# The first stage of a hybrid convolution, scan and spectral kernel: the order of a planner against an order written out in the program

## The chip, the cores and the metric

The kernel runs on one core of one Trainium2 chip. The metric is device time in microseconds of one launch, as the median of several runs. A core has five engines with instruction queues of their own: PE (TensorE; PEld are its weight loads), DVE (VectorE), ACT (ScalarE), POOL (GpSimd) and SP (SyncE), which here issues all the transfers. Each engine works through its queue in order; it waits for others through semaphores.

## The reference, cut to what matters

The layer computes, in float32, on 4 images of 128 channels and 64 x 64 pixels:

```python
# layer 0, on the group-normalized image (groups of 4 channels)
feat = gelu(dwconv2d(x, conv1_w, conv1_b))                  # 3x3, per channel
ca = sigmoid(relu(feat.mean((2, 3)) @ ca1_w.T) @ ca2_w.T)   # a gate for each channel
feat = gelu(dwconv2d(feat * ca[:, :, None, None], conv2_w, conv2_b))
scores = sigmoid(einsum('bchw,oc->bohw', feat, head_w)[:, 0] + head_b[0])
final_scores = 0.7 * scores + 0.3 * sigmoid(10 * var(x, axis=channels, ddof=1))
sm = final_scores.reshape(B, 16, 4, 16, 4).mean((2, 4))     # 256 patches of 4 x 4
idx = argsort(-sm)                                          # patches in order of their score
# tokens (x + pe), layer-normalized, taken in that order, then a scan over them,
# an output projection, and back into the image's order
# layer 1: a second scan over 512-wide chunks and a spectral convolution, with
# filters M_phi_plus[i], M_phi_minus[i], M_u[i] of four branches i
y_soft = softmax(log_weights + gumbel)                      # weighs the four branches
```

The change lies in the part up to the ordered tokens, and in a preparation for layer 1: the four branches' filter matrices are scaled by the branch weights and added up.

## The kernel before

The kernel is a chain of three stages, written with a tile framework that gives out buffers from pools and puts in the waits. `layer0_front` is the first stage, `layer0_scan` the second, `layer1` the third. In stages two and three the program switches the framework's planner off (`tc.manual_schedule()`), so that each engine's queue has the program's order. In `layer0_front` the planner is on: it chooses the order of every queue.

`layer0_front` loops over the 4 images (`for b in range(NB)`). For each image:

- SP loads the image, `xs` (128 x 4096). DVE takes its statistics (`bn_stats`, L126), PE averages them over groups of four channels (`gs`), POOL raises to the power -0.5 (`rs`, L142), and DVE writes the normalized image into the bordered tile `xg` (L144).
- ACT lays the pixels out by patches (`xp1`, L149). PE transposes them, four 128 x 128 blocks at a time (`tp`, L164). For each of these eight blocks of four, DVE adds the position code (`x1`, L166) and takes statistics of both (`stx`, `st1`, L168 and L169). 64 aggregates follow (L171, L172), a `pow` on POOL (`r1`, L176), the product `m1` on DVE (L180), and 32 scalings of `x1` on ACT (L183).
- A convolution (`conv`, L94 to L109) has eight pieces of 128 x 512. In each, PE does four of the nine taps as products with diagonal matrices into a PSUM tile (L104) and DVE the other five as a chain of accumulates (L106): the first one reads the PSUM tile and writes an SBUF tile `sum`, of which there are three; the other four read and write `sum`. ACT applies a Gelu to `sum`. The first convolution's pieces give `f1`, with channel sums (L193).
- A small chain makes the gate: `mean`, `hid`, `hs`, `cap`, `ca` (L198 to L207). The gate is multiplied into the second convolution's weights (`d2b`, `w2b`). The second convolution gives `f2` (L215).
- PE makes the scores by 32 products (`sc`, L225); ACT and DVE finish them (L230 to L237). DVE ranks the 256 patches by comparison (L243 to L259) and writes the permutation `perm`. PE transposes it for later (L263), gathers the tokens in order by 32 products with it (`ranked`, L274), ACT evacuates (`xn`, L277), SP stores `xnt`.

Tiles of one tag share buffers. In pool `xp` every tag has one buffer (`xp1` and `f2` share the tag `patches`). PSUM pool `pm` has four buffers of one bank each, for the pieces of convolution, the transposes and the gathers; `ps1` has two.

`spectral_weights` is a generator that `layer0_front` advances with `next(matrices, None)`, six times at the start of each image but the first. Each step makes the summed filter matrices of one of 16 filters: SP loads `raw`, ACT does four scalings (L677), POOL three adds, a sum and a difference (L679, L695, L696), SP stores two `pq`. Ahead of them it makes the branch weights and the matrices `mue` from `mu` in one piece. The planner decides where these instructions lie in the queues; in the profile all of them are beside image 0.

Of the kernel before, what the change touches and what calls it, by code (L numbers as in the profile page):

```python
# [15 lines left out]
NB = 4  # L16
L = 4096
# [6 lines left out]
def layer0_front(ctx: ExitStack, tc, ident, half, w, x, xnt, perm_t, pqd, mud):  # L24
# [3 lines left out]


    nc = tc.nc  # L30
    cp = ctx.enter_context(tc.tile_pool(name="a_c", bufs=1))
    xp = ctx.enter_context(tc.tile_pool(name="a_x", bufs=1))
    sm = ctx.enter_context(tc.tile_pool(name="a_sm", bufs=2))
    pm = ctx.enter_context(tc.tile_pool(name="a_pm", bufs=4, space=PSUM))
    ps1 = ctx.enter_context(tc.tile_pool(name="a_p1", bufs=2, space=PSUM))

    def load(name, shape, src):
# [77 lines left out]
    matrices = spectral_weights(  # L115
        ctx, tc, w["sigma"], w["M_u"], w["M_phi_plus"], w["M_phi_minus"], w["log_weights"], w["gumbel"], pqd, mud
    )
    for b in range(NB):

        xs = xp.tile([128, L], F32, tag="xs", name="xs")  # L120
        nc.sync.dma_start(xs, x[b])
        for _ in range(6 if b else 0):
            next(matrices, None)
        st = sm.tile([128, 8, 6], F32, tag="st", name="st")
        for q in range(8):
            nc.vector.bn_stats(st[:, q, :], xs[:, bass.ts(q, 512)])  # L126
        mv = sm.tile([128, 2], F32, tag="mv", name="mv")
        nc.vector.bn_aggr(mv, st)

        gm = sm.tile([128, 1], F32, tag="gm", name="gm")  # L130
        sq = sm.tile([128, 1], F32, tag="sq", name="sq")
# [8 lines left out]
        nc.vector.tensor_scalar(sq, gs, 1e-5, None, ALU.add)  # L140
        rs = sm.tile([128, 1], F32, tag="rs", name="rs")
        nc.gpsimd.tensor_tensor(rs, sq, half[:, 0:1], ALU.pow)  # L142
        xg, inside = bordered("xg")
        nc.vector.tensor_scalar(  # L144
            inside, xs.rearrange("c (y x) -> c y x", x=64), gm, rs, ALU.subtract, ALU.mult
        )
        xp1 = xp.tile([128, L], F32, tag="patches", name="xp1")
        for oy in range(4):
            nc.scalar.copy(  # L149
                by_patch(xp1, oy), inside[:, oy::4, :].rearrange("c py (px ox) -> c py px ox", ox=4)  # L150
            )


        x1 = xp.tile([128, 2, 16, 128], F32, tag="x1", name="x1")
        stx = sm.tile([128, 2, 16, 6], F32, tag="stx", name="stx")
        st1 = sm.tile([128, 2, 16, 6], F32, tag="st1", name="st1")
        mvx = sm.tile([128, 2, 16, 2], F32, tag="mvx", name="mvx")
# [2 lines left out]
        for h in range(2):  # L160
            for oy in range(4):
                tp = pm.tile([128, 4, 128], F32, tag="mm", name="tp")
                for ox in range(4):
                    nc.tensor.transpose(tp[:, ox, :], patches[:, h, 4 * oy + ox, :], ident)  # L164
                o4 = bass.ts(oy, 4)
                nc.vector.tensor_tensor(x1[:, h, o4, :], tp, pe[:, h, o4, :], ALU.add)  # L166
                for o in range(4):
                    nc.vector.bn_stats(stx[:, h, 4 * oy + o, :], tp[:, o, :])  # L168
                    nc.vector.bn_stats(st1[:, h, 4 * oy + o, :], x1[:, h, 4 * oy + o, :])  # L169
            for o in range(16):  # L170
                nc.vector.bn_aggr(mvx[:, h, o, :], stx[:, h, o, :])  # L171
                nc.vector.bn_aggr(mv1[:, h, o, :], st1[:, h, o, :])  # L172
# [5 lines left out]
        )  # L178
        m1 = sm.tile([128, 2, 16], F32, tag="m1", name="m1")
        nc.vector.scalar_tensor_tensor(m1, mv1[:, :, :, 0], -1.0, r1, ALU.mult, ALU.mult)  # L180
        for h in range(2):
            for o in range(16):
                nc.scalar.activation(  # L183
                    x1[:, h, o, :], x1[:, h, o, :], AF.Identity, bias=m1[:, h, o : o + 1],
                    scale=r1[:, h, o : o + 1],
                )


        f1, inside1 = bordered("f1")
# [1 line left out]
        for i in range(8):  # L191
            h, oy = divmod(i, 4)
            nc.scalar.activation(  # L193
                inside1[:, 32 * h + oy : 32 * h + oy + 29 : 4, :], conv(xg, d1, w1, h, oy), AF.Gelu, bias=b1,
                accum_out=sums[:, i : i + 1],
            )
        mean = sm.tile([128, 1], F32, tag="mean", name="mean")
        nc.vector.tensor_reduce(mean, sums, AX, ALU.add)  # L198
        nc.vector.tensor_scalar(mean, mean, 1.0 / L, None, ALU.mult)
# [5 lines left out]
        nc.tensor.matmul(cap, ca2, hs, start=True, stop=True)  # L205
        ca = sm.tile([128, 1], F32, tag="ca", name="ca")
        nc.scalar.activation(ca, cap, AF.Sigmoid)  # L207
        d2b = xp.tile([128, PT, 128], F32, tag="d2b", name="d2b")
        nc.vector.tensor_scalar(d2b, d2, ca, None, ALU.mult)
        w2b = sm.tile([128, 9], F32, tag="w2b", name="w2b")  # L210
        nc.vector.tensor_scalar(w2b, w2, ca, None, ALU.mult)
        f2 = xp.tile([128, L], F32, tag="patches", name="f2")
        for i in range(8):
            h, oy = divmod(i, 4)
            nc.scalar.activation(  # L215
                by_patch(f2, oy)[:, 8 * h : 8 * h + 8],
                conv(f1, d2b, w2b, h, oy).rearrange("c py (px ox) -> c py px ox", ox=4), AF.Gelu, bias=b2,
            )


        sc = ps1.tile([128, 2, 16], F32, tag="one", name="sc")
        fpatch = f2.rearrange("c (h p o) -> c h o p", h=2, o=16)
        for h in range(2):
            for o in range(16):
                nc.tensor.matmul(  # L225
                    sc[:, h, o : o + 1], fpatch[:, h, o, :], head,
                    start=True, stop=True,
                )
        s1 = sm.tile([128, 2, 16], F32, tag="s1", name="s1")
        nc.scalar.activation(s1, sc, AF.Sigmoid, bias=head_b)  # L230
        s2 = sm.tile([128, 2, 16], F32, tag="s2", name="s2")
# [3 lines left out]
        score = sm.tile([128, 2], F32, tag="score", name="score")  # L235
        nc.vector.tensor_reduce(score, s1, AX, ALU.add)
        nc.vector.tensor_scalar(score, score, 1.0 / 16, None, ALU.mult)  # L237


        row = ps1.tile([128, 2, 128], F32, tag="one", name="row")  # L240
        for h in range(2):
# [6 lines left out]
        for h in range(2):  # L248
            more = sm.tile([128, 1], F32, tag="more", name="more")
            same = sm.tile([128, 1], F32, tag="same", name="same")  # L250
            junk = sm.tile([128, 256], F32, tag="junk", name="junk")
            mine = score[:, h : h + 1]
            nc.vector.tensor_scalar(junk, scores, mine, None, ALU.is_gt, ALU.add, accum_out=more)
            junk = sm.tile([128, 256], F32, tag="junk", name="junk")
            nc.vector.scalar_tensor_tensor(
                junk, scores, mine, before[:, h, :], ALU.is_equal, ALU.mult, accum_out=same
            )
            nc.vector.tensor_tensor(more, more, same, ALU.add)
            nc.vector.tensor_scalar(perm[:, h, :], index, more, None, ALU.is_equal)  # L259
        for h in range(2):  # L260
            tp = ps1.tile([128, 2, 128], F32, tag="one", name="tp1")
            for k in range(2):
                nc.tensor.transpose(tp[:, k, :], perm[:, k, bass.ts(h, 128)], ident)  # L263
            nc.vector.tensor_copy(perm_t[:, b, h, :], tp.rearrange("p k j -> p (k j)"))


        xn = xp.tile([128, 3 + L], F32, tag="xn", name="xn")
        nc.vector.memset(xn[:, 0:3], 0.0)
        ranked = xn[:, 3:].rearrange("c (r o) -> c o r", o=16)
        for o in range(0, 16, 2):  # L270
            ps = pm.tile([128, 2, 256], F32, tag="mm", name="ranked")
            for i in range(2):
                for h in range(2):
                    nc.tensor.matmul(  # L274
                        ps[:, i, :], x1[:, h, o + i, :], perm[:, h, :], start=h == 0, stop=h == 1
                    )
            nc.scalar.activation(ranked[:, o : o + 2, :], ps, AF.Identity, bias=nb, scale=ng)  # L277
        nc.sync.dma_start(xnt[b], xn)


NS = 16
# [344 lines left out]
def spectral_weights(ctx, tc, sigma, m_u, m_plus, m_minus, log_w, gumbel, pqd, mud):  # L626
# [19 lines left out]
    nc.vector.tensor_scalar(lw, lw, top, None, ALU.subtract)  # L646
    soft = cp.tile([128, 4], F32, name="soft")
    tot = cp.tile([128, 1], F32, name="tot")
    nc.scalar.activation(soft, lw, AF.Exp, accum_out=tot)
    nc.vector.reciprocal(tot, tot)  # L650
    nc.vector.tensor_scalar(soft, soft, tot, None, ALU.mult)
# [22 lines left out]
    def branch_sums(dst, src, weight):  # L674

        for i in range(4):
            nc.scalar.activation(dst(3 - i), src(i), AF.Copy, scale=weight(i))  # L677
        for i in range(1, 4):
            nc.gpsimd.tensor_tensor(dst(3 - i), dst(3 - i), dst(4 - i), ALU.add)  # L679

    mu = mp.tile([128, 4, 3, 128], F32, name="mu", bufs=1)
    for i in range(4):
        nc.sync.dma_start(mu[:, i], m_u[i].rearrange("k d e -> d k e"))
    mue = mp.tile([128, 4, 3, 128], F32, name="mue", bufs=1)
    branch_sums(lambda r: mue[:, r], lambda i: mu[:, i], lambda i: wt[:, i : i + 1])
    nc.sync.dma_start(mud, mue)
    yield
    for k in range(NK):
        raw = mp.tile([128, 2, 4, 128], F32, tag="raw", name="raw")
        nc.sync.dma_start(raw[:, 0], m_plus[:, k].rearrange("i d e -> d i e"))  # L690
        nc.sync.dma_start(raw[:, 1], m_minus[:, k].rearrange("i d e -> d i e"))
        sums = mp.tile([128, 2, 4, 128], F32, tag="sums", name="sums")
        branch_sums(lambda r: sums[:, :, r], lambda i: raw[:, :, i], lambda i: both[:, i, k : k + 1])
        pq = mp.tile([128, 2, 4, 128], F32, tag="pq", name="pq")
        nc.gpsimd.tensor_tensor(pq[:, 0], sums[:, 0], sums[:, 1], ALU.add)  # L695
        nc.gpsimd.tensor_tensor(pq[:, 1], sums[:, 0], sums[:, 1], ALU.subtract)  # L696
        for side in range(2):
            nc.sync.dma_start(pqd[k, side], pq[:, side])
        yield
# [673 lines left out]
```

## Time and profile before

| what | us |
|---|---|
| median of 3 runs | 21742.6 |
| lowest and highest run | 21742.6, 21744.73 |
| the profiled execution | 21746.66 |
| its span | 21744.9 |
| first stage: from the start to the last evacuation of `xn` | 607.5 |
| from one `xg` to the next (27.1, 201.5, 337.5, 472.3) | 174.4, 136.0, 134.8 |
| DVE, POOL, PE, ACT busy over the whole span | 20628.6, 20221.1, 17469.3, 15865.3 |
| DVE, PE, ACT, POOL busy in the first 640 us | 409.3, 428.3, 213.8, 126.2 |

The profile is of one execution. A span is the time from its first to its last instruction. In a group of instructions the columns are line, engine, operation, tiles out and in, shapes and number, then busy time in us and the mean of one in ns, then the idle time ahead of them and what ended it. In a timeline a row is start and length in us; instructions of one engine can overlap by a fraction, so lengths from start to start are the better measure of a queue. The first stage is 2.8% of the span.

### The profile page before, as it was taken

To read this page: it belongs to the slowest core of one execution; us is meant where nothing else is said; L and a number is where in the kernel's file an instruction comes from. 1 tells how busy PE (TensorE), PEld (TensorE's weight loads), DVE (VectorE), ACT (ScalarE), POOL (GpSimd) and SP (SyncE) were. 2 spreads that over 40 slices of the span, in tenths; PEclk is the share of its full clock that TensorE was granted. 3 is DMA by queue.
4 is the path that set the end of the run, shared out by engine and by line. 5 is a ranking of instruction groups with operands and counts; after the bars stand their busy time and mean duration, and the time that the engine had idled before them with its cause. 6 is when DMAs were issued, how large, how long until landed. Compare 5 with 4: busy or idle time off the path is not lost.

```text
span 21744.9 us, 291339 instructions
## 1 busy us (share of the span) xinstructions
PE 17469.3 (80%) x98516; PEld 7646.0 (35%) x98516; DVE 20628.6 (95%) x11808; ACT 15865.3 (73%) x29216; POOL 20221.1 (93%) x5679
## 2 busy tenths in 40 slices
PE   6788854565858888877768888869498899999999
PEld 3344421222323333333323333324143344434344
DVE  6788889999999999999999999999999999999993
ACT  3677767777777777777777777777777777877773
POOL 2677789999999999999999999999999999999993
PEclk7999966776979999998879999979699999999999
DMA  1455544555757777766667777757476777777775
GB/s 68 112 139 141 140 149 151 173 178 163 217 171 219 219 222 220 218 205 196 201 189 218 222 218 220 222 183 231 154 235 216 226 235 235 234 232 231 232 227 150
DMA packets 2420940, 4245.65 MB, mean 195 GB/s; under 512 B 795208, under 2 KB 1255024, under 8 KB 2416368
## 3 DMA queue, kind: packets, MB, share of 16 engines
q1 hardware_dynamic: 2419440, 4227.01, 63.6%
q8 instruction: 776, 12.71, 0.2%
q14 instruction: 724, 5.93, 0.1%
HBM read 3605.76 MB, written 620.24 MB: 194 GB/s over the span
## 4 chain that ended last, share of the span: by engine, by line
DVE 51%; POOL 23%; PE 9%; ACT 8%; issue 6%; DMA 2%; SPq 0%; DVEq 0%; POOLq 0%; ACTq 0%
DVE s L1155 44%; POOL v L1143 22%; ACT da L1152 5%; PE conv L1103 4%; DVE states L513 3%; DVE p L517 1%; PE yp L1172 1%; ACT f L505 1%; PE fin L1047 1%; PE y L529 1%; DMA dlb<-delta 1%; PE mm L422 1%; DMA yd<-ye 1%; PE conv L104 0%; DVE sum L106 0%
## 5 line engine op out<-in xcount | busy, mean ns | idle before, releaser
L1143 POOL TENSOR_TENSOR v<-u,dlb 128x2044 f32<-128x2044 f32 x4096 | 18333.8, 4536 | 68.1 <-DMA dlb<-delta 64.9
L1155 DVE TENSOR_TENSOR_SCAN s<-da,v 128x1024 f32<-128x1024 f32 x8192 | 18130.6, 2272 | 192.7 <-ACT da L1152 91.1
L1152 ACT ACTIVATE da<-dlb,at 128x511 f32<-128x511 f32 x16384 | 11302.4, 690 | 2235.1 <-DVE s L1155 1774.2
L1103 PE MATMUL conv<-strip,tok 128*128 128x512 f32 (+3 forms) x20480 | 8609.0, 550 | 5.9 <-DMA strip<-in_phi 5.8
L1172 PE MATMUL yp<-s,c 128*32 128x256 f32 x65536 | 5030.9, 438 | 3065.5 <-DVE s L1155 1601.6
L1103 PEld LDWEIGHTS conv<-strip,tok 128*128 128x128 f32 x20480 | 3666.5, 191 | 4104.4 <-issue 3705.1
L1172 PEld LDWEIGHTS yp<-s,c 128*32 128x32 f32 x65536 | 1992.5, 121 | 6865.7 <-issue 1822.2
L1147 ACT COPY v<-vf 128x4 f32<-128x4 f32 x4096 | 812.7, 198 | 2234.0 <-DVE s L1155 2228.7
L491 POOL TENSOR_TENSOR v<-dx,bcb 128x1024 f32<-128x1024 f32 x512 | 1207.2, 2358 | 433.6 <-DVE states L513 427.3
L1047 PE MATMUL fin<-conved,pq 128*128 128x512 f32 (+1 forms) x3200 | 1411.8, 536 | 11.1 <-ACT sum L1068 4.1
L513 DVE TENSOR_TENSOR_SCAN states<-f,v 128x1024 f32<-128x1024 f32 x512 | 1175.9, 2297 | 176.1 <-ACT f L505 126.5
L505 ACT ACTIVATE f<-dt,an 128x255 f32<-128x255 f32 x2048 | 973.6, 476 | 420.0 <-DVE states L513 369.2
L1178 ACT COPY ye<-yp 128x512 f32<-128x512 f32 x2048 | 1185.0, 579 | 16.7 <-PE yp L1172 15.4
L529 PE MATMUL y<-p,ident 128*128 128x512 f32 x2048 | 1004.8, 619 | 152.3 <-DVE p L517 147.4
L1114 ACT COPY conved<-conv 128x512 f32<-128x512 f32 x1344 | 778.0, 579 | 327.7 <-PE conv L1103 326.4
L517 DVE TENSOR_TENSOR p<-states,bcb 128x1024 f32<-128x1024 f32 x512 | 627.0, 1225 | 38.2 <-PE y L535 0.4
L529 PEld LDWEIGHTS y<-p,ident 128*128 128x128 f32 x2048 | 368.3, 195 | 684.0 <-issue 356.3
L1047 PEld LDWEIGHTS fin<-conved,pq 128*128 128x128 f32 x3200 | 528.0, 193 | 221.3 <-issue 160.7
L422 PE MATMUL mm<-ow,yg 128*32 128x128 f32 x2048 | 280.5, 296 | 106.8 <-ACT om L426 105.3
L1063 DVE TENSOR_TENSOR xo<-xo,fin 128x512 f32<-128x512 f32 x32 | 21.3, 667 | 306.8 <-PE fin L1055 306.8
L422 PEld LDWEIGHTS mm<-ow,yg 128*32 128x32 f32 x2048 | 235.3, 138 | 212.5 <-ACT om L426 128.4
L356 PE MATMUL mm<-xin,taps 128*128 128x512 f32 x512 | 237.2, 606 | 28.3 <-DVE f L335 14.0
(242 smaller groups left out, 5932.4 us busy)
## 6 DMA issues: line engine op xcount, KB each, us to landing
dlb<-delta SPq DMA_DIRECT2D x4096, 512.0 KB, 4.1
strip<-in_phi SPq DMA_DIRECT2D x1536, 448.0 KB, 4.8
yd<-ye SPq DMA_DIRECT2D x2048, 256.0 KB, 4.1
bcb<-bcd SPq DMA_DIRECT2D x1024, 256.0 KB, 4.2
strip<-in_phi SPq DMA_DIRECT2D x1024, 256.0 KB, 4.4
pq<-pqd SPq DMA_DIRECT2D x1088, 64.0 KB, 3.8
yt<-yd SPq DMA_DIRECT2D x4096, 4.0 KB, 3.4
pq<-pqd SPq DMA_DIRECT2D x256, 128.0 KB, 4.0
```

Of the source, the lines that this page charges most:

```text
L491: nc.gpsimd.tensor_tensor(v, ready[n][2][:, :, bass.ts(i, SUB)].unsqueeze(1).broadcast_to((128, 2, 2, SUB)), bc[:, 0].unsqueeze(2).broadca ...
L505: nc.scalar.activation(factors[j % 2][:, a, k, 1:], ready[n][1][:, k, SUB * i + 1 : SUB * i + SUB], AF.Exp, scale=an[:, k, 2 * g + a : 2 * ...
L513: nc.vector.tensor_tensor_scan(states.rearrange(flat), factors[j % 2].rearrange(flat), v.rearrange(flat), 0.0, ALU.mult, ALU.add)
L517: nc.vector.tensor_tensor(p, states, bc[:, 1].unsqueeze(2).broadcast_to((128, 2, 2, SUB)), ALU.mult)
L529: nc.tensor.matmul(t.rearrange("p k t -> p (k t)"), ident, p[:, a].rearrange("p k t -> p (k t)"), start=g == 0 and a == 0, stop=False, ski ...
L1047: nc.tensor.matmul(fin[:, bass.ds(c0, w)], pq[:, n, :], u[:, bass.ds(c0, w)], start=begin and n == 0, stop=end and not partly, skip_group_ ...
L1103: nc.tensor.matmul(ps[:, skip:], tok[:, 1 - r if side else r, j, :], strip[:, bass.ds(c0 - lo, TS - skip)], start=src == sources[0] and j ...
L1143: nc.gpsimd.tensor_tensor(v[:, :, :, 1:], ready[0][:, :, 1:].unsqueeze(1).broadcast_to((128, VD, 2, TS - 1)), dl[:, :, 1:].unsqueeze(2).br ...
L1152: nc.scalar.activation(da[:, h, 1:], dl[:, d % VD, 1:], AF.Exp, scale=at[:, h, d : d + 1])
L1155: nc.vector.tensor_tensor_scan(s[:, d % GD].rearrange("p h t -> p (h t)"), da.rearrange("p h t -> p (h t)"), v[:, d % VD].rearrange("p h t ...
L1172: nc.tensor.matmul(yp[i // 2][bass.ts(q, 32), i % 2], c[:, h, t], s[:, :, h, t], start=h == 0, stop=h == 1)
L1178: nc.scalar.copy(ye, yp[j].rearrange("p i d t -> p i t d"))
```

## The change

The planner is switched off in `layer0_front`, and the order is written out. The loop's body becomes two generators: `tokens(b)`, from the load of `xs` to `m1`, and `ordered(b, ...)`, from the first convolution to the store. A small class advances them by pieces. Image 0's `tokens` runs whole; then for each image its `ordered` pieces alternate with the `tokens` pieces of the next image and with steps of `matrices`:

```python
    first = Pieces(tokens(0))
    first.go()
    for b in range(NB):
        rest = Pieces(ordered(b, *first.result))
        first = Pieces(tokens(b + 1)) if b + 1 < NB else Pieces(iter(()))
        first.go(1)                 # load of the next image
        for _ in range(4):
            rest.go(2)              # two pieces of the first convolution
            next(matrices, None)
        first.go(1)                 # statistics of the next image
        rest.go(2)                  # gate
        first.go(1)                 # its group sums and pow
        rest.go(4)                  # gate into the weights; three pieces of the second convolution
        first.go(1)                 # xg and the layout by patches
        next(matrices, None)
        rest.go(6)                  # five pieces, eight scores
        for n in (1, 1, 1, 1, 1, 1, 2, 2):
            first.go(1)             # four transposes with their statistics
            rest.go(n)              # scores, score arithmetic, ranking, permutation, gathers
        first.go()
        rest.go()
```

The order in which each engine gets its instructions follows from this. On DVE, behind the last accumulate of the second convolution, it is: four blocks of statistics, the score arithmetic, 32 aggregates and a block, the ranking, a block, the permutation's copies, a block, a block, 32 aggregates, `m1`. On ACT four of the 32 scalings of `x1` stand behind each Gelu of the first convolution, and four scalings of a filter behind every second one. On SP the load of the next image stands behind the store of the last one.

Buffers: `pm` has six instead of four. `xs` has 3 + 4096 columns and shares its buffer with `xn`; `xp1`, `f2` have their own; `x1` has two.

```diff
-    pm = ctx.enter_context(tc.tile_pool(name="a_pm", bufs=4, space=PSUM))
+    pm = ctx.enter_context(tc.tile_pool(name="a_pm", bufs=6, space=PSUM))
...
-        xs = xp.tile([128, L], F32, tag="xs", name="xs")
+        xs = xp.tile([128, 3 + L], F32, tag="xs", name="xs")[:, 0:L]
...
-        xp1 = xp.tile([128, L], F32, tag="patches", name="xp1")
+        xp1 = xp.tile([128, L], F32, tag="xp1", name="xp1")
...
-        x1 = xp.tile([128, 2, 16, 128], F32, tag="x1", name="x1")
+        x1 = xp.tile([128, 2, 16, 128], F32, tag="x1", name="x1", bufs=2)
...
-        for h in range(2):
-            for o in range(16):
-                nc.scalar.activation(
-                    x1[:, h, o, :], x1[:, h, o, :], AF.Identity, bias=m1[:, h, o : o + 1],
-                    scale=r1[:, h, o : o + 1],
-                )
+            for o in range(4 * i, 4 * i + 4):
+                h, o = divmod(o, 16)
+                nc.scalar.activation(
+                    x1[:, h, o, :], x1[:, h, o, :], AF.Identity, bias=m1[:, h, o : o + 1],
+                    scale=r1[:, h, o : o + 1],
+                )
+            yield
...
-        f2 = xp.tile([128, L], F32, tag="patches", name="f2")
+        f2 = xp.tile([128, L], F32, tag="f2", name="f2")
...
-        xn = xp.tile([128, 3 + L], F32, tag="xn", name="xn")
+        xn = xp.tile([128, 3 + L], F32, tag="xs", name="xn")
```

In `spectral_weights` a step is taken ahead of the softmax, the matrices `mue` are made in three slices through the buffers of the filters, and each filter's `raw` is loaded one filter ahead:

```diff
+    yield
     nc.scalar.activation(soft, lw, AF.Exp, accum_out=tot)
...
-    mu = mp.tile([128, 4, 3, 128], F32, name="mu", bufs=1)
-    for i in range(4):
-        nc.sync.dma_start(mu[:, i], m_u[i].rearrange("k d e -> d k e"))
-    mue = mp.tile([128, 4, 3, 128], F32, name="mue", bufs=1)
-    branch_sums(lambda r: mue[:, r], lambda i: mu[:, i], lambda i: wt[:, i : i + 1])
-    nc.sync.dma_start(mud, mue)
-    yield
-    for k in range(NK):
+    for k in range(3):
+        raw = mp.tile([128, 2, 4, 128], F32, tag="raw", name="mu")[:, 0]
+        nc.sync.dma_start(raw, m_u[:, k].rearrange("i d e -> d i e"))
+        sums = mp.tile([128, 2, 4, 128], F32, tag="sums", name="mue")[:, 0]
+        branch_sums(lambda r: sums[:, r], lambda i: raw[:, i], lambda i: wt[:, i : i + 1])
+        nc.sync.dma_start(mud[:, :, k], sums)
+
+    def fetch(k):
         raw = mp.tile([128, 2, 4, 128], F32, tag="raw", name="raw")
         nc.sync.dma_start(raw[:, 0], m_plus[:, k].rearrange("i d e -> d i e"))
         nc.sync.dma_start(raw[:, 1], m_minus[:, k].rearrange("i d e -> d i e"))
+        return raw
+
+    ahead = fetch(0)
+    yield
+    for k in range(NK):
+        raw, ahead = ahead, fetch(k + 1) if k + 1 < NK else None
```

## The prediction

> **What bounds the kernel now.** The change touches only the first stage: read instruction by instruction, the built kernels agree on every engine behind the last `xnt` store. So I cut out the chain of waits of the first 700 us. Start, length, what:
>
> ```profile
> 472.26 2.43 DVE xg L144
> 474.76 1.07 ACT xp L149
> 475.87 1.13 PE tp L164 x4
> 477.03 0.69 DVE x L166
> 499.58 5.41 POOL r L176
> 505.24 12.43 ACT x L183 x32
> ...
> 540.16 30.73 PE conv L104 x64
> 570.89 13.66 PE sc L225 x64
> 586.11 1.24 PE row L244 x4
> ...
> 591.95 14.29 PE ranked L274 x62
> 606.27 1.21 ACT xn L277
> ```
>
> This is image 3, and images 1 and 2 look the same: a serial run through normalize, transpose and statistics on DVE, a `pow` on POOL, two convolutions, scores, ranking, gathers. From one `xg` to the next are 136.0 and 134.8 us, and the last image takes 135.2. No engine is full in it. The first image is longer. The busy times of the two stretches (PE, PEld, DVE, ACT, POOL):
>
> ```profile
> 201.50:337.50 136.00, 105.43 (x304) 63.42 (x304) 92.47 (x268) 43.79 (x75) 6.00 (x2) 0.77 0.08 31
> 27.00:201.50 174.50, 105.56 (x304) 63.03 (x304) 126.64 (x287) 73.63 (x144) 102.72 (x86) 0.73 0.35 114
> ```
>
> POOL's 102.7 us there are the spectral weights, all 16 of them, which the scheduler puts beside image 0. What they do to DVE is in the groups of that stretch, then of image 2 (337.5 to 472.3), where POOL is idle:
>
> ```profile
> L106 DVE SCALAR_TENSOR_TENSOR sum<-f,w2b,sum 128x512 f32<-128x512 f32 x32 | 41.5, 1307 | 0.8
> L106 DVE SCALAR_TENSOR_TENSOR sum<-f,w2b,conv 128x512 f32<-128x512 f32 x8 | 5.9, 737 | 8.8 <-PE conv L104 5.8 <-ACT f L215 3.0
> ```
>
> ```profile
> L106 DVE SCALAR_TENSOR_TENSOR sum<-f,w2b,sum 128x512 f32<-128x512 f32 x32 | 23.6, 750 | 0.8
> ```
>
> The same accumulate is 1307 ns beside POOL and 750 without it; the form whose second operand is in PSUM stays at 737. Last, the timeline of DVE at the start of the second convolution of image 2:
>
> ```profile
> 411.04 0.75 DVE L106 SCALAR_TENSOR_TENSOR sum<-f,w2b,conv 128x512 f32<-128x512 f32 x1 [5.65 <-PE conv L104]
> 411.82 3.11 DVE L106 SCALAR_TENSOR_TENSOR sum<-f,w2b,sum 128x512 f32<-128x512 f32 x4
> 414.85 0.74 DVE L106 SCALAR_TENSOR_TENSOR sum<-f,w2b,conv 128x512 f32<-128x512 f32 x1
> ```
>
> A piece of convolution written in plain order costs DVE 3.81 us (411.04 to 414.85) and waits 5.65 us for PE's first piece. Where the scheduler interleaves two pieces, as in the first convolution, the same ten take 6.67 (384.96 to 391.63), 3.3 each.
>
> **What the Trainium skill says.** SBUF — State Buffer, section "Who interferes with whom": a DVE instruction with two SBUF inputs contends with a GpSimd instruction that reads SBUF, one with a single SBUF input does not. The trace agrees (1307 and 750 against 737). TensorE: Matmul & The Clock Gate, section "What's actually happening": an idle array restarts at half clock for some 3.4 us. The trace agrees in kind: the first piece of a convolution takes 5.65 us, the later ones about 3.7 (29.91 us for 8). Perfetto Trace Analysis, section "Optimization Strategy": regimes with different bottlenecks may gain from interleaving. That is what is done here; how far it pays is the question.
>
> **The change, part by part.** Durations are start to start from the timelines of the profiled execution (us).
>
> *Taken off the path.* Image b+1's normalize, transposes and statistics move under image b. Today the front costs from 472.26 to 505.2, 33.0, and is followed by the first convolution. Three fronts go (images 1 to 3); image 0's stays as it is, up to 60.6. Counted: 8 blocks of one add and eight statistics, 2.15 each; 2 times 32 aggregates, 2.13; `xg` 2.9 with its border; 4 ACT copies of 1; 5.45 `pow`.
>
> *What the tail becomes.* Take t = 0 at the last accumulate of the second convolution. Gelu to 0.85; PE has the first 16 scores behind it, does 8 scores (3.4), 4 transposes (0.7), 8 scores, and then the transposes for block 4, so DVE's blocks end at 2.15, 4.3, 7.35 and 11.5. Score arithmetic to 12.4, aggregates 14.5, block 5 to 16.65, diagonal and PE `row` to 18.3, ranking to 21.3. PE: permutation transposes and block 7's to 23.3, gathers and block 8's to 38.5 (62 gathers take 14.07 in image 2), the next convolution's first piece 42.2, DVE starts at 42.3. DVE's own blocks, the wait for `pow` (5.45, in front of `m1`) and the border end at 38.4: the stall is hidden behind the gathers. Today: 440.34 to 472.26 is 31.9, then the front of 33.0. So 64.9 become 42.3.
>
> *Given back.* (a) DVE's queue is now in plain order: 8 pieces of the first convolution at 3.81 are 30.5 (bunched today: 32.4 with 5.2 of next statistics in it). (b) Those statistics (5.2) stand behind it and the next image's group sums on PE and DVE inside the gate's chain: 9.3 from the last accumulate to PE's next start, against 3.1 today after the Gelu. (c) The second convolution has `xg` in its queue, which waits for POOL's `rs`, already there: 5.7 + 8 x 3.81 + 2.9 = 39.1, and 41.6 with a weight beside it (below); today 35.1. (d) The spectral weights are spread, five to an image. One keeps POOL for about 6.5 (3.43 + 1.6 + 1.6), in which DVE's piece of 3.81 becomes 6.4 (119.83 to 126.26), a loss of 2.6. Three fall into the first convolution (7.8), the fourth behind its last Gelu, into the gap, one into the second convolution (2.6). Their ACT part (4 x 0.4) and the 32 scalings of `x1` (12.4), now four behind each Gelu, fit: 3.2 a piece against DVE's 3.8. Nothing is behind them but ACT's own Gelus, and three `sum` tiles cover them.
>
> Period of images 1 and 2: 38.3 + 9.3 + 41.6 + 42.3 = 131.5, against 135.4: 4 gained each.
>
> *Image 0.* Its first convolution meets the weights' setup. DVE waits some 4 for ACT's softmax exponential behind the fourth Gelu, then 4 of small operations (to 84.5). The three slices of `mu` go one after another: SP is in order, and each load stands behind the previous slice's store, which waits for POOL. Per slice ACT 1.6, POOL 1.5, issue 0.5 to 1, landing 3.7: about 8. ACT reaches its fifth Gelu at 103 instead of 85; DVE, three pieces ahead, stalls from 96. With the two loads of weight 0 behind it, PE starts the second convolution at 117.7, today at 107.1. Then 41.6 + 42.3: DVE starts image 1's first convolution at 201.6, where today `xg` begins at 201.5 and that convolution's bulk at 234.3. 33 gained so far.
>
> *Image 3.* No front beside it: 38.3 + 4.5 + 36.2 (5.7 + 30.5) + 30.6 (scores 7, ranking 6, gathers 16, evacuation) = 109.6. Today from the same point (505.2) to 607.5 is 102.3: 7.3 lost, by plain order and contention.
>
> *SP's queue.* `xs` of image b+1 shares its buffer with `xn` of b-1, so its load waits for that store (8.0 in the chain), and the weights' loads queue behind it. It has the 38 of a first convolution; the loads are one weight ahead. I cost this at nothing; without that cover it would be the landing, 9.2. The layer-1 weight loads move ahead of the second `xs` and take the place of `mu`'s 0.8 MB: nothing. Table loads stay four an image. PSUM's six buffers instead of four only let PE run ahead.
>
> Sum: stage end 201.6 + 2 x 131.5 + 109.6 = 574.2, against 607.5: 33 less. The profiled execution is 21746.66 (span 21744.9), hence 21713; the median of the runs is 4.1 lower, so **21710**.
>
> The cost that the trace doesn't show is contention when weights trickle in. Lower bound 1 per weight (POOL waiting for ACT in between), upper 3.3 (piece at 6.4, and POOL itself at 8 when both fight): 13 weights, so -21 to +9 on the sum; I take 2.6 because it was measured with POOL full. The plain piece could be 3.56, as at 425 to 436, where only one operation is interleaved: up to 16 less over 64 pieces; slower than 3.81 has no reason with PE ahead, bar PE's clock (0.73 to 0.81 granted here). The `mu` chain: 8 either way.
>
> **The rivals.** *Better cover* (30 in 100). Contention 1.4 per weight and pieces at 3.6: 33 + 16 + 13 = 62 gained, 21681. For it: POOL shows idle gaps as soon as ACT feeds it singly. Against: the contended pieces of image 0 are steadily 5.8 to 6.4 long.
>
> *ACT starved by the weights* (8 in 100), the slower case. Each weight's four scalings stand between Gelus. In image 0 today ACT waits for loads:
>
> ```profile
> L677 ACT ACTIVATE sums<-raw,both 128x256 f32<-128x256 f32 x64 | 27.8, 496 | 50.4 <-DMA raw<-in_M_phi_minus 28.1 <-POOL pq L696 11.9 <-POOL pq L695 7.1
> ```
>
> A load is issued behind the store of two weights earlier: POOL 6.7, two stores 2, two loads 1, landing 3.7 and ACT 1.7 make 15 for two weights, and DVE's four pieces give 15 to 20. If the stores hold SP as the pairs at 135 and 161 did (7 to 9), each weight is late by 5 and a Gelu, then DVE, with it: 16 x 5 = 80 lost, 47 net, 21790. It decides from 4.8 per weight. Against: those long stores came when SP had four in a row waiting for POOL.
>
> *No change at all* (within the middle case): if the tail's interleaving costs PE or DVE some 8 more per image, 33 shrinks to nothing, 21743.
>
> **How the numbers follow.** Some 0.2% (43 us) is what a measurement of this kernel can tell from no change. My forecast (62 in 100) gains 10 to 43, within it; better cover gains 44 to 75; starved loses over 43. Hence 0.30 faster, 0.62 same, 0.08 slower; the range 21670 to 21750 leaves out the starved case and the ends of the others.
>
> **What would show it.** In the changed profile: `xg` of images 1 to 3 inside the second convolution; DVE `sum` starting about 201, 333 and 464; 42 between a second convolution's end and the next first; last `xn` near 574; accumulates near 1.3 us only beside POOL; ACT waiting for `mu` twice, 5 each. Wrong if ACT waits for `raw` at most weights, if the tail is over 48, or if spans behind the stage differ by over 10.

## The result and the profile after

| us | before | after |
|---|---|---|
| median, 18 runs each | 21745.47 | 21705.62 |
| lowest to highest | 21741.26 to 21753.52 | 21699.14 to 21713.26 |
| profiled execution (span) | 21746.66 (21744.9) | 21708.22 (21706.5) |
| last `xn` evacuated | 607.5 | 562.7 |
| span behind that point | 21137.4 | 21143.8 |

The ratio is 0.9982 (95% interval 0.9975 to 0.9988): 40 us or 0.18% less. Forecast were 21710 and a stage end of 574.2. The time is met within 5 us, but by misses that partly cancel: the stage gained 44.8 instead of 33, and the rest of the program shows 6 more in the profile, where nothing was forecast. The forecast also started from a median of 21742.6, of 3 runs, where 18 runs give 21745.47; as a gain, 33 was forecast and 40 came. That the time was met so closely is in part luck.

In the changed kernel `conv` accumulates at L107 (before L106), PE multiplies at L105, scores at L237, gathers at L289. The chain of waits of the first 700 us, cut down (start, length, what):

```profile
176.23 4.12 PE ranked L289 x16
180.79 10.36 PE ranked L289 x48
191.16 3.48 PE conv L105 x8
...
233.03 4.76 DVE st L127 x8
...
242.74 5.20 PE conv L105 x8
...
495.42 29.35 PE conv L105 x64
524.77 13.66 PE sc L237 x64
...
545.61 15.81 PE ranked L289 x64
561.45 1.21 ACT xn L292
```

Behind a gather comes the next image's convolution at once (191.16). Where `xg`, layout, transposes and `pow` stood before, 33 us, nothing is left. New on the chain are the next image's statistics, 4.76 at 233.03, in front of the gate. In the last image PE, not DVE, is the path of the second convolution (29.35 us in one stretch).

From one first accumulate to the next (columns: PE, PEld, DVE, ACT, POOL busy, clock, DMA share, GB/s):

```profile
194.66:323.19 128.53, 96.74 (x305) 60.96 (x304) 106.01 (x268) 51.56 (x95) 35.72 (x27) 0.79 0.21 74
```

128.5 against 136.0 before, although POOL is now busy for 35.7 in every period instead of 6.0: the spectral sums lie in all of them and not in the first alone. Their mark is in the groups of accumulates of this stretch, then in the timeline of DVE:

```profile
L107 DVE SCALAR_TENSOR_TENSOR sum<-xg,w,sum 128x512 f32<-128x512 f32 x32 | 31.9, 996 | 1.1
L107 DVE SCALAR_TENSOR_TENSOR sum<-f,w2b,sum 128x512 f32<-128x512 f32 x32 | 26.2, 820 | 1.1
```

```profile
203.06 3.11 DVE L107 SCALAR_TENSOR_TENSOR sum<-xg,w,sum 128x512 f32<-128x512 f32 x4
206.09 0.74 DVE L107 SCALAR_TENSOR_TENSOR sum<-xg,w,conv 128x512 f32<-128x512 f32 x1
206.87 5.73 DVE L107 SCALAR_TENSOR_TENSOR sum<-xg,w,sum 128x512 f32<-128x512 f32 x4
```

Four accumulates take 3.11 without a filter beside them and 5.73 with one: 2.62 more. The first convolution has three such pieces (32 x 0.246 = 7.9), the second not quite one (2.2).

### The profile page after: what moved, and what is told of

It reads as the page before. It is cut to its first block, busy times and chain, and to the rows that moved or that the text cites. A ratio compares the mean times of both kernels' runs of the same rounds, so it can differ in the third digit from the quotient of the medians.

```text
span 21706.5 us, 291342 instructions
## 1 busy us (share of the span) xinstructions
PE 17459.7 (80%) x98516; PEld 7665.7 (35%) x98516; DVE 20644.4 (95%) x11808; ACT 15868.1 (73%) x29225; POOL 20223.0 (93%) x5685
## 4 chain that ended last, share of the span: by engine, by line
DVE 51%; POOL 23%; PE 9%; ACT 8%; issue 6%; DMA 2%; SPq 0%; DVEq 0%; POOLq 0%; ACTq 0%
DVE s L1212 44%; POOL v L1200 22%; ACT da L1209 5%; PE conv L1160 4%; DVE states L563 3%; DVE p L567 2%; PE yp L1229 1%; ACT f L555 1%; DVE sum L107 1%; PE fin L1104 1%; PE y L579 1%; DMA dlb<-delta 1%; PE mm L472 0%; DMA yd<-ye 0%; PE ranked L289 0%
```

## The experiments

"Theory" is the reading of the prediction: interleaving takes the front off the path, plain order and spread filters give some back. Stage end is the end of the last evacuation of `xn` in the profile; the rest is the span behind it. Each ratio is against the kernel before, run alongside (medians 21745.47 to 21747.8). The run "no POOL sums" leaves out a part of the work; all others do all of it.

| run | median us (runs) | ratio, 95% interval | stage end | rest |
|---|---|---|---|---|
| before | 21745.47 (18) | | 607.5 | 21137.4 |
| after | 21705.62 (18) | 0.9982, 0.9975 to 0.9988 | 562.7 | 21143.8 |
| serial | 21755.17 (12) | 1.0003, 0.9995 to 1.0012 | 619.9 | 21136.0 |
| no POOL sums | 21672.19 (5) | 0.9967, 0.9954 to 0.9980 | 531.3 | 21142.2 |
| filters in the tail | 21691.75 (10) | 0.9975, 0.9966 to 0.9984 | 552.8 | 21137.1 |
| buffers, planner on | 21812.1 (7) | 1.0030, 1.0019 to 1.0042 | 668.0 | 21140.3 |
| pairs | 21706.41 (15) | 0.9981, 0.9973 to 0.9988 | 562.7 | 21143.3 |
| `mu` ahead | 21699.37 (11) | 0.9978, 0.9969 to 0.9986 | 557.5 | 21136.2 |
| tail, pairs, `mu` | 21684.58 (7) | 0.9970, 0.9959 to 0.9981 | 545.2 | 21136.9 |
| four PSUM buffers | 21707.21 (1) | | 563.0 | 21142.5 |
| filters in the gaps | 21679.83 (7) | 0.9970, 0.9959 to 0.9981 | 537.7 | 21140.4 |

**The written order without interleaving.** The same chains, one image after the other, and before's buffers for `xs`, `xn` and `x1`.

```diff
-        first.go(1)
-        rest.go(2)
-        first.go(1)
-        rest.go(4)
-        first.go(1)
-        next(matrices, None)
         rest.go(6)
-        for n in (1, 1, 1, 1, 1, 1, 2, 2):
-            first.go(1)
-            rest.go(n)
-        first.go()
+        next(matrices, None)
         rest.go()
+        first.go()
```

> The changed kernel with the same written order inside an image, the same weight steps and the planner off, but the next image's tokens run only behind the last gathers (its load stays early, and xn has a buffer of its own for that). Theory (the gain is the overlap of the next image's front with this image's tail): the front of 33 us comes back between the gathers and the convolution, the tail without blocks is about 31, the second convolution loses its xg (2.9) and the gate its statistics (5). Period near 38 + 6 + 38 + 31 + 33 = 146 instead of 129, three times: the end of the first stage moves from 563 to about 613, the total to about 21757. Rival (the gain is the planner's bad order and the spread of the weights, not the overlap): end of stage within 10 us of 563, total about 21710.

Measured: 619.9, period 146.7. Plain order with the filters spread loses 12.4 against the planner; the interleaving, with the buffers that it needs, gains 57.2 on top (619.9 to 562.7). The change's gain is the difference of two larger terms, as the prediction had it. The 12.4 need not be the plain order's: the filters cost some 10 us in a period (7.9 and 2.2 by the accumulates of after, above), and 146.7 less 10 is an estimate of 137 without them, close to the planner's 136.0 and 134.8, which had no filter beside them. No run here separates the two.

**The contention.** POOL's five operations per filter, and its three per slice of `mu`, are taken away.

```diff
-        for i in range(1, 4):
-            nc.gpsimd.tensor_tensor(dst(3 - i), dst(3 - i), dst(4 - i), ALU.add)
...
-        pq = mp.tile([128, 2, 4, 128], F32, tag="pq", name="pq")
-        nc.gpsimd.tensor_tensor(pq[:, 0], sums[:, 0], sums[:, 1], ALU.add)
-        nc.gpsimd.tensor_tensor(pq[:, 1], sums[:, 0], sums[:, 1], ALU.subtract)
+        pq = sums
```

> The changed kernel without the adds, sums and differences of the spectral weights on POOL (left out; ACT's scalings, the loads and the stores stay, the scaled values are stored as they are). Theory (POOL's work slows the accumulates with two SBUF inputs): every accumulate at 0.76 us, each piece 3.81 instead of 6.4 beside a weight; per image 3 x 2.6 in the first convolution and some 2.2 in the second: 4 x 7.8 + 3 x 2.2 = about 33 to 37 less, end of stage near 528, total near 21671. Rival (ACT's scalings or the transfers slow DVE): accumulates stay at 1.4 us beside the weights, end of stage within 5 of 563.

Measured: 531.3, that is 31.4 less than after. The accumulates of image 1's first convolution in this run:

```profile
L107 DVE SCALAR_TENSOR_TENSOR sum<-xg,w,sum 128x512 f32<-128x512 f32 x32 | 24.1, 752 | 1.1
```

996 became 752, and loads, stores and ACT's scalings stayed. So 31.4 us is what the sums cost where the change puts them, and the time followed (33 less in the median). Not all of it is contention. In image 0 the store of a slice of `mu`, and the next slice's load behind it, no longer wait for POOL, and ACT reaches the fifth Gelu 5.1 earlier than in after (99.45). In this run:

```profile
94.36 0.73 ACT L194 ACTIVATE f<-sum,b 128x512 f32<-128x512 f32 x1
```

PE starts image 0's second convolution at 109.4 instead of 114.3. These 5 us belong to the chain of `mu`; some 26 are left for the contention with DVE.

**Filters in the tail.** After image 0's setup, four filters an image beside statistics and ranking, none beside the accumulates.

```diff
-        for _ in range(4):
+        for i in range(4):
             rest.go(2)
-            next(matrices, None)
+            if b == 0 and i < 2:
+                next(matrices, None)
...
-        next(matrices, None)
         rest.go(6)
-        for n in (1, 1, 1, 1, 1, 1, 2, 2):
+        for i, n in enumerate((1, 1, 1, 1, 1, 1, 2, 2)):
             first.go(1)
             rest.go(n)
+            if i in (0, 1, 3, 5):
+                next(matrices, None)
```

> The changed kernel with the weight steps moved: the first two (setup) stay behind pieces 2 and 4 of image 0, the 16 filters stand four to an image behind the first, second, fourth and sixth block of transposes, where DVE does statistics with one SBUF input. Theory (the price is port contention with two-input accumulates, so it depends on what DVE does then): the convolutions lose their slow pieces, 30 to 35 us in sum; POOL's weights at 4.8 us each, 19 per image, fit the tail of 39 ahead of the pow; the gathers wait for ACT at most 3. End of stage near 532, total near 21676. Rival (the weights cost the same wherever they stand, since the tail is bound by DVE as well and its ranking and statistics slow down, or ACT's evacuations come late): end of stage 555 to 570.

Missed: 552.8, only 9.9 of 31.4. The groups of DVE between 280 and 320 us, first of after, then of this run, show where the rest went:

```profile
L273 DVE TENSOR_SCALAR perm<-index,more 128x256 f32<-128x256 f32 x2 | 0.7, 353 | 0.1
L272 DVE TENSOR_TENSOR more<-more,same 128x1 f32<-128x1 f32 x2 | 0.3, 160 | 0.1
```

```profile
L273 DVE TENSOR_SCALAR perm<-index,more 128x256 f32<-128x256 f32 x2 | 1.7, 835 | 0.1
L272 DVE TENSOR_TENSOR more<-more,same 128x1 f32<-128x1 f32 x2 | 1.3, 626 | 0.1
```

Statistics and aggregates keep their times (a block 2.18, an aggregate 0.15), but the score arithmetic and the ranking, which every gather waits for, are held up. An operation on 128 numbers that takes 160 ns alone takes 626. From the second convolution to the next first one, PE's starts moved apart by 2 to 4 us per image; from the first to the second they moved together by 8.6. In the last image 7.8 are gained before the second convolution and 7.0 lost behind it, 6 of them between the scores and the permutation's transposes (12.2 instead of 6.3).

**Is it the buffers?** The kernel before, planner on, with the buffers and the spectral steps of after.

```diff
-    pm = ctx.enter_context(tc.tile_pool(name="a_pm", bufs=4, space=PSUM))
+    pm = ctx.enter_context(tc.tile_pool(name="a_pm", bufs=6, space=PSUM))
...
-        xs = xp.tile([128, L], F32, tag="xs", name="xs")
+        xs = xp.tile([128, 3 + L], F32, tag="xs", name="xs")[:, 0:L]
...
-        xn = xp.tile([128, 3 + L], F32, tag="xn", name="xn")
+        xn = xp.tile([128, 3 + L], F32, tag="xs", name="xn")
```

(`xp1`, `f2`, `x1` and `spectral_weights` are taken over too.)

> The kernel before, planner on and its own loop, with the changed kernel's buffers (pm six, x1 two, xs with xn, xp1 and f2 apart) and its spectral_weights. Theory (the order has to be written: the planner goes by the program's priority and puts the next image behind this one): periods stay near 135, end of stage 595 to 612, total 21735 to 21750. Rival (buffers were what held the planner back, so with two x1 it overlaps by itself): end of stage 560 to 575, total near 21707.

Missed, on the slow side: 668.0. Its chain of waits between image 0 and image 1:

```profile
195.66 1.21 ACT xn L277
196.88 6.32 DMA xnt<-xn
203.22 7.37 DMA xs<-in_x
210.61 4.86 DVE st L126 x8
...
218.66 2.42 DVE xg L144
```

The shared buffer puts store, load and statistics on the path in each image, 21.8 from 196.88 to 218.66. The same pair exists in after (SP issues the store at 192.44 and the load at 198.72), but a first convolution, in which nothing needs `xs`, covers it until 233.03. In the planner's order the buffers are a loss; the written order makes them usable.

**Pairs.** Two pieces' accumulates alternate on DVE, with four `sum` tiles and one buffer for `perm`.

```diff
+        for tap in range(PT, 9):
+            for ps, sum_, rows in out:
+                nc.vector.scalar_tensor_tensor(
+                    sum_, rows[tap], taps[:, tap : tap + 1], ps if tap == PT else sum_, ALU.mult, ALU.add
+                )
```

> The changed kernel with the accumulates of two pieces of a convolution interleaved on DVE (a fourth sum tile, one perm instead of two for its room). Theory (in plain order every accumulate waits for the one in front, 0.78 from start to start, alternating ones start after 0.66): a pair takes 6.7 instead of 7.6, but PE gives a pair in 6.9 to 7.4, so about 0.2 to 0.4 a piece where POOL is idle; a pair also makes ACT's Gelus come in twos and the first piece later. 64 pieces, some 15 of them beside POOL: 10 to 18 less, end of stage 545 to 553, total about 21692. Rival (PE or the hand-over bounds the pieces): end of stage within 4 of 563.

The rival held: 562.7, no gain. In the timeline of DVE the pair is faster, and then DVE waits:

```profile
198.32 0.75 DVE L112 SCALAR_TENSOR_TENSOR sum<-xg,w,conv 128x512 f32<-128x512 f32 x1 [2.71 <-PE conv L108]
198.98 5.38 DVE L112 SCALAR_TENSOR_TENSOR sum<-xg,w,sum 128x512 f32<-128x512 f32 x8
...
205.24 0.75 DVE L112 SCALAR_TENSOR_TENSOR sum<-xg,w,conv 128x512 f32<-128x512 f32 x1 [0.21 <-PE conv L108]
```

205.24 - 198.32 = 6.92 for two pieces instead of 7.62, but that is also PE's pace (two pieces of 3.48 are 6.96), and the first pair waits 2.71 for its second piece. A pair with no filter beside it saves 0.7, so four save about what the wait took: in image 3's second convolution the accumulates take 30.3 from first to last, in after 30.6.

**`mu` ahead.** All three slices are loaded before the softmax, POOL's `pow` for `sig` is moved ahead of it, and the filters' `fetch` is defined before this loop.

```diff
+    two = [mp.tile([128, 2, 4, 128], F32, tag="raw", name="mu") for _ in range(2)]
+    mu = [two[0][:, 0], two[0][:, 1], two[1][:, 0]]
+    for k in range(3):
+        nc.sync.dma_start(mu[k], m_u[:, k].rearrange("i d e -> d i e"))
...
     for k in range(3):
-        raw = mp.tile([128, 2, 4, 128], F32, tag="raw", name="mu")[:, 0]
-        nc.sync.dma_start(raw, m_u[:, k].rearrange("i d e -> d i e"))
+        raw = mu[k]
```

> The changed kernel with the three slices of mu loaded together ahead of the softmax, the first filter behind the second slice, and sigma's pow ahead too. Theory (image 0's first convolution is held by ACT in front of a chain of three loads behind stores): the waits of ACT for mu (7.1 and 5.6) and of DVE for sigma (3.0) and Gelu 5 (3.0) go; the second convolution of image 0 starts near 105 instead of 114.3, end of stage near 553, total near 21697. Rival (the loads of filters 0 and 1 behind them then bound it): less than 4 gained.

About half: PE starts image 0's second convolution at 109.2 (after: 114.3) and the stage ends 5.2 earlier. The fifth Gelu starts at 89.96 instead of 99.45 and DVE no longer waits for it. But POOL's sums, the slices' and the first filter's, now meet DVE's accumulates and not its waits.

**The three together**: the edits of tail, pairs and `mu` in one kernel.

> Weights in the tail, interleaved pairs and mu ahead together. If the three costs are independent: 31 + 20 (pairs pay at all 64 pieces once POOL is quiet) + 9 = 60 below the changed kernel, end of stage near 503, total near 21646, some 0.45% below the kernel before. If they overlap (PE becomes the bound of the convolutions, or ACT that of the tail): end of stage 515 to 535.

Missed: 545.2. It is what tail and `mu` give added up (562.7 - 9.9 - 5.2 = 547.6), and pairs add little here too. It was still 21 us faster than after.

**Four PSUM buffers**, a single run.

```diff
-    pm = ctx.enter_context(tc.tile_pool(name="a_pm", bufs=6, space=PSUM))
+    pm = ctx.enter_context(tc.tile_pool(name="a_pm", bufs=4, space=PSUM))
```

> The changed kernel with four buffers in pm instead of six. Theory (PE runs ahead of DVE, two pieces are enough): end of stage within 3 of 563. Rival (transposes of the next image share the pool with the pieces of convolution and with the gathers, so PE waits for DVE in the tail): end of stage 570 or later.

The stage ends at 563.0: the two extra buffers do nothing.

**Filters in the gaps**, from what the tail run taught, with `mu` ahead and without pairs.

```diff
+        if b in (1, 2):
+            next(matrices, None)
-        for _ in range(4):
+        for i in range(4):
             rest.go(2)
-            next(matrices, None)
+            if b == 0 or i == 3:
+                next(matrices, None)
...
-        next(matrices, None)
+        if b == 0:
+            next(matrices, None)
         rest.go(6)
-        for n in (1, 1, 1, 1, 1, 1, 2, 2):
+        for i, n in enumerate((1, 1, 1, 1, 1, 1, 2, 2)):
             first.go(1)
             rest.go(n)
+            if i == 6 or i == (7 if b == 3 else 0):
+                next(matrices, None)
```

> The filters are moved to where DVE waits or takes statistics only: in each image one beside the gate, one beside the first two statistics blocks of the tail, one beside the gathers; in images 1 and 2 one more before the first piece of the convolution; two in image 0's convolutions. The mu slices are loaded ahead as in the run with mu ahead; no pairs. Theory (the spectral sums cost what they cost because DVE's two-input accumulates and the small score and ranking operations run beside POOL, and nothing where DVE waits or reads one SBUF operand): of the 31 us that all sums cost only some 8 are left (2.6 twice, 1.5 twice), so the stage ends near 557.5 - 23 = 534, and the time is near 21673, below the best version so far. Rival (any filter in the tail moves the cost to what the tail waits for, as when four went there): about the 10 us of that run, the stage ends near 547 and the time is near 21685, the same as the best version so far.

The theory held within 4 us: the stage ends at 537.7, with the lowest median of all versions that do the whole work, 21679.83, 26 below after (its lead over the three together, 5, is less than the spread of the runs). The base of its sum was too large, though: of the 31 us, 5 are the chain of `mu`, which the loads ahead had already won. Of the some 26 that were left it saved 19.8 (557.5 to 537.7). POOL's timeline, then DVE's, at the start of image 1's tail:

```profile
271.69 2.35 POOL L740 TENSOR_TENSOR sums<-sums 128x256 f32<-128x256 f32 x3 [39.81 <-ACT sums L738]
274.12 1.27 POOL L762 TENSOR_TENSOR pq<-sums 128x512 f32<-128x512 f32 x1
```

```profile
272.14 0.67 DVE L169 TENSOR_TENSOR x<-tp,pe 128x512 f32<-128x512 f32 x1
...
274.30 0.68 DVE L169 TENSOR_TENSOR x<-tp,pe 128x512 f32<-128x512 f32 x1
```

A filter passes beside a block of statistics and neither gives way: the block is 2.16 long, as without it. This agrees with the Trainium skill, SBUF — State Buffer, section "Who interferes with whom": with at most one SBUF input, and outside its two-port modes, DVE stays on ports of its own. The slow `perm` of the tail run, 835 ns, agrees with it as well: the section counts `tensor_scalar` among those that can take both port pairs and then block with GpSimd, which a count of its SBUF inputs alone would not have told.

## Why the prediction was right, and where not

The mechanism was right: from the first accumulate of image 1 on, the fronts are gone and the first convolution follows the gathers. The sizes, step by step:

| step | forecast | measured |
|---|---|---|
| first accumulate of image 0 | 60.6 | 58.7 |
| PE starts image 0's second convolution | 117.7 | 114.3 |
| that start to the last accumulate, images 0 to 2 | 41.6 each | 41.5, 40.4, 41.0 |
| tail, images 0 to 2 | 42.3 each | 38.9, 40.0, 40.3 |
| first convolution to the last accumulate | 38.3 | 38.4 |
| gate | 9.3 | 9.7 |
| contention of one filter | 2.6 | 2.62 |
| period of images 1 and 2 | 131.5 | 128.5, 129.4 |
| image 3, first accumulate to the end | 109.6 | 110.1 |
| behind the stage | 0 | +6.4 in the profile |

**The tail of image 0 was over-priced by 3.4.** The prediction let only the first 16 scores be done ahead of the last Gelu, so that the third group of eight, and behind it the transposes of blocks 3 and 4, came after it: the blocks were to end at 2.15, 4.3, 7.35 and 11.5. That was wrong: the third group reads only the fifth and sixth piece of `f2` (two of the four pixel rows of a patch, lower half), which are ready before. The timeline of PE around the last accumulate (155.79):

```profile
152.65 3.45 PE L237 MATMUL sc<-head,f 128*128 128x1 f32 x16
155.96 1.10 PE L167 MATMUL tp<-ident,xp 128*128 128x128 f32 x4
156.85 3.45 PE L237 MATMUL sc<-head,f 128*128 128x1 f32 x16
```

24 of 32 scores are done by 156.1 and only the last eight follow the last Gelu. DVE's four blocks start at 155.79, 157.96, 160.11 and 162.27, without a wait, and the score arithmetic at 8.6 behind the last accumulate instead of 11.5. That is 2.9 of the 3.4. Another 0.2 is PE's first piece behind the gathers: it takes 3.48, where the prediction took 3.7, its figure for the later pieces, which is the mean of all eight with the slow first one (29.91 / 8). In image 1 the tail is 1.1 longer than in image 0: the first 16 gathers take 5.27 instead of 4.12, at a granted clock of 0.66 against 0.85 in these stretches.

**The start of image 0's second convolution was put 3.4 too late.** Image 0's first accumulate came 1.9 earlier than forecast; the other 1.5 lies in the chain of `mu` and in the gate behind it. The timeline of ACT:

```profile
89.99 1.28 ACT L728 ACTIVATE mue<-mu,wt 128x128 f32<-128x128 f32 x4 [7.11 <-DMA mu<-in_M_u]
96.86 1.28 ACT L728 ACTIVATE mue<-mu,wt 128x128 f32<-128x128 f32 x4 [5.59 <-issue]
...
99.45 0.73 ACT L194 ACTIVATE f<-sum,b 128x512 f32<-128x512 f32 x1
```

The slices came 8.4 and 6.9 apart, and the fifth Gelu at 99.45 instead of 103. DVE, which had also waited 3.01 for POOL's `pow` (not foreseen), then stood still for 2.97 where 7 were forecast. What the chain costs was shown by loading ahead, 5 us, and again by the run without POOL's sums.

**Sum.** Image 1's first accumulate starts 6.9 earlier than forecast (3.4, 0.1 and 3.4). The two periods give 3.0 and 2.1: in image 1 the tail 2.3 and the second convolution 1.2, less 0.5 for the gate and the first convolution. The last image takes back 0.5: 11.5, the whole error of the stage end.

**Behind the stage** nothing was to change, and the profile of after shows 6.4 more (the medians say 5: 44.8 gained in the stage, 39.9 in the time). At the first `states` of stage two the lead is 44.4, at the first scan of stage three 40.7, at the end 38.4: it melts slowly, with no place of its own. In the other kernels the rest is 21136.0 to 21143.3, in no order that follows an edit, while runs of one kernel differ by 12 to 14. What sets it stays open.

**The rivals.** "ACT starved" did not occur: in the list of ACT's waits from 190 to 562 us none is for a load. SP issues image 2's `xs` at 198.72 and a filter's `raw` at 199.1, and the next filter's scalings run without a wait. "Better cover" asked for a gain of 44 to 75: the stage alone just reached that (44.8), the time did not (40), and its reasons did not hold: contention was 2.62, not 1.4, and a plain piece took 3.81, not 3.6. The gain beyond forecast came mostly from the tails (7.7 of 11.5).

## What to carry to other kernels

Before moving work onto an idle engine, list what runs beside it on the engine that shares its ports, each operation with the memories that it reads: here one filter's sums on POOL cost 2.6 us beside accumulates of two SBUF operands and up to 0.9 us in a single tiny operation of the score and ranking chain, and nothing beside statistics or waits. Order written by hand pays only through what it overlaps: here the plain order with the filters spread lost 12 us and the overlap won 57. And when pieces of work are alternated, ask of each group which piece it really needs last, not which is issued before it.

## What the runs showed of the hardware that was not expected

- Size does not protect an operation from contention. `more` (128 x 1, two SBUF inputs) went from 160 to 626 ns in the mean, the score's 128 x 32 product from 192 to 1105. Such a delay is less than one of POOL's instructions, the longest of which, the 128 x 512 sum, takes about 1.3 us there.
- The first convolution after the gathers needs no run-up of PE: its first piece takes 3.48, against 5.20 behind the gate. The granted clock was 1.00 in the gathers before it (48 in 10.36 us) and in that piece, and 0.71 in the piece behind the gate.
